# Sending the first unit's rows to the expert table one by one, with its routing closer behind its mLSTM

## The chip, the cores and the metric

The kernel runs on one core of a Trainium2 chip, in one launch. The metric is the time of an execution on the device in microseconds (us). Five engines work side by side, each through its own instructions in order: TensorE (PE, with its weight loads shown as PEld), VectorE (DVE), ScalarE (ACT), GpSimd (POOL) and SyncE (SP), which here only issues DMAs. POOL issues DMAs too, the indirect ones.

## The reference

One decoder layer over 16 sequences of 256 tokens with 256 channels, in float32:

```python
x = x + attention(layernorm(x), W_qkv, W_out)     # causal, 16 heads of 16 channels
x = x + mlstm(layernorm(x), ctx, ctx, ...)        # causal, 8 heads of 32 channels, gated decay
x = x + moe(layernorm(x), router_w, router_b, expert_up, expert_down)

def moe(x):                                       # 4096 tokens, 8 experts, hidden width 1024
    probs = softmax(x @ router_w + router_b)
    top_w, top_idx = top_k(probs, 2)
    comb = sum(top_w * one_hot(top_idx))
    return sum_e comb[:, e] * (gelu(x @ up[e].T) @ down[e].T)
```

Attention and mLSTM work sequence by sequence. The experts work on tokens: each token goes to two of the eight.

## The kernel before

**Stages.** The 16 sequences form two groups of 8 and four units of 4. The attention runs over `k`, a sequence times four quads of heads (64 in all, and four more values of `k` until the pipeline is empty): `attend_next(k)` computes the maxima of quad `k`, the weights of quad `k - 2` (scores `ps_st`, exponentials `p` on ACT, L408) and the values of quad `k - 4` (`ps_av`, L419 and L424). Between weights and values, `diagonals` (L340) applies the causal mask with two `affine_select` instructions on POOL (L343). The mLSTM's decay weights `d` pass through the same `diagonals`.

**The mLSTM and the routing** of a group are lists of steps that `mixing(group, slow)` (L915) writes out. A round `i` takes one half (four heads) of a sequence; `lags` (L961) says how many rounds later each step follows:

```python
end = [(4, finish), (2, values2)] if slow else [(2, values2), (3, finish)]
lags = ((1, scores2), *end, (5, layer3), (7, scale3), (8, turn3), (9, logits))
```

`finish` adds the mLSTM's result to x. `layer3` (L685) takes the statistics of the third layer norm and writes x to the output `out_x` by a DMA of SP's (L696). `scale3` (L702) normalizes x in place (L708, on POOL for the first group), and so must wait until that DMA has read it. `turn3` transposes it and `logits` multiplies it by the router (L727). When the last sequence of a unit has its logits, `logits_by_token`, `softmax3`, `choose` (a series of small DVE instructions) and `count` (`ps_n`, L797) give every token its two slots in a table in DRAM, one region for each expert.

**The table.** `send` (L826) is one indirect DMA on POOL (L827): 128 rows of 265 floats (the token, its expert weights and its number) to 128 slots. A unit has 8 tiles with two slots each, so 16 sends; `send_unit` (L837) does the two of one tile. After a unit's last send comes its `plan` (L846), which gives out blocks of 128 or 256 slots of an expert. `load_rows` (L1101) fetches a block's rows from the table; it must wait for the sends that came before its plan.

**What runs beside what.** The first group's attention runs alone (k = 0 to 35). Beside the second group's attention (k = 36 to 67), `take_evenly` (L1036) deals out the steps of the first group's mLSTM and routing, in equal numbers to each k, and ends two k before the attention's end (`EARLY`). `mixing` returns its list in parts. For the first group the cut `part` lies behind the first unit's plan; what is behind it (`kept`, L1059) is done after the attention, alternating with the first steps of the second group (`begin`, L1191). After the attention come the experts' blocks: 48 of them, each with up matmuls (`ps_u`, L1153), gelu, down matmuls (`ps_d`, L1171) and an indirect DMA that adds the result to the output (L1176). The steps of the second group are dealt out between their matmuls:

```python
parts = [(0, FIRST - 6, begin), (FIRST - 6, SECOND - 3, rest), (SECOND - 3, THIRD - 3, end)]
```

With FIRST = 9, SECOND = 13 and THIRD = 21, `begin` lies beside blocks 0 to 2, `rest` beside 3 to 9 and `end` beside 10 to 17. The remaining blocks run with no mLSTM beside them.

**Order on the engines.** In the stage of the blocks the orders of PE, ACT and SP are those of the program text. Everywhere else a planner puts the instructions of each engine in order at compile time, by the order of the text and by when its costs say that an instruction can start; a dependence between two instructions keeps their order. `bank`, `four` and others look at the list `singles`, which is empty until the attention is closed.

Of the kernel before, what the change touches and what calls it, by code (L numbers as in the profile page):

```python
# [34 lines left out]
UT = UB * SC  # L35
# [35 lines left out]
def decoder_layer(  # L71
# [15 lines left out]
    nc = tc.nc  # L87
# [65 lines left out]
    table = dram.tile([E * REGION + TB, ROW], F32, tag="table", name="table")  # L153
# [8 lines left out]
    def statistics(b, mv, rstd):  # L162

        for c in range(SC):
            st = lstm.tile([P, 6], F32, tag="st", name="st", bufs=4)
            nc.vector.bn_stats(st, xtile(b, c))
            nc.vector.bn_aggr(mv[:, c, :], st)
        nc.vector.tensor_scalar(rstd, mv[:, :, 1], LN_EPS, None, ALU.add)
        nc.scalar.activation(rstd, rstd, AF.Ln)
        nc.scalar.activation(rstd, rstd, AF.Exp, scale=-0.5)  # L170

    def normalized(xn, b, mv, rstd, engine=nc.gpsimd):
        for c in range(SC):
            engine.tensor_scalar(  # L174
                xn[:, c, :], xtile(b, c), mv[:, c, 0:1], rstd[:, c : c + 1], ALU.subtract, ALU.mult
            )
# [15 lines left out]
    singles = []  # L192
# [56 lines left out]
    for i in range(2):  # L249

        v = big.tile([P, SC, NA, HP], F32, tag=f"v{i}", name=f"v{i}")
# [26 lines left out]
    def step(f, *args):  # L278
        return lambda: f(*args)
# [3 lines left out]

    seq, quads = {}, {}

    def start1(b):
        mv = lstm.tile([P, SC, 2], F32, tag="mv1", name="mv1")
        rstd = lstm.tile([P, SC], F32, tag="rstd1", name="rstd1")
        statistics(b, mv, rstd)
        xn = lstm.tile([P, SC, D], F32, tag="xn", name="xn", bufs=3)  # L290
        normalized(xn, b, mv, rstd, nc.gpsimd if b else nc.vector)
        seq[b] = {"xn": xn}
# [47 lines left out]
    def diagonals(p):  # L340

        for block in (p[:, :, :P], p[:, :, S:]):
            nc.gpsimd.affine_select(  # L343
                out=block, in_=block, compare_op=ALU.is_ge, fill=0.0, base=0,
                pattern=[[0, 4], [1, P]], channel_multiplier=-1,
            )

    def maxima(k):

# [331 lines left out]
    routed = {}  # L681
# [144 lines left out]
    def send(place, row):  # L826
        i = nc.gpsimd.indirect_dma_start(  # L827
            out=table, out_offset=bass.IndirectOffsetOnAxis(ap=place, axis=0), in_=row, in_offset=None,
            bounds_check=E * REGION - 1, oob_is_err=False,
        )  # L830
        for other in sent:
            tc.declare_no_dep(i.ins, other, reason="the slots of any two rows differ")
        for other in fetched:
            tc.declare_no_dep(i.ins, other, reason="blocks given out before have no slot that was still free")
        sent.append(i.ins)

    def send_unit(u, c0, c1):  # L837
        g, t0 = divmod(u * UT, GB * SC)
        source = xs[g].rearrange("p b c r -> p (b c) r")
        for i in range(c0, c1):  # L840
            for k in range(2):
                send(routed[u]["place"][:, k, i : i + 1], source[:, t0 + i, :])

    plans, blk = {}, {}

# [69 lines left out]
    def mixing(group, slow):  # L915


        b0, b1 = group * GB, (group + 1) * GB
        ready = b0 + UB
        u = b0 // UB  # L920

        def pause(n):
            return [None] * (n if slow else 0)

        first = [step(load2, b) for b in range(b0, ready)] + [step(start2, b0)]
        for b in range(b0, ready):
            if b + 1 < ready:
                first.append(step(start2, b + 1))
            first.append(step(turn2, b))
        first += [step(gates, u), None, None] + pause(4) + [step(gates_out, u), step(gates_by_token, u), None]  # L930
        first += [step(maxima2, b0)] + pause(2)


        units = [[(b, dc) for b in range(v * UB, (v + 1) * UB) for dc in range(DC)] for v in (u, u + 1)]
        gap = [(None, None)] * (GAP if slow else 0)
        halves = units[0] + gap + units[1]
        n, n0 = len(halves), len(units[0]) + len(gap)
        second = {
            0: [(load2, ready), (start2, ready)],
            1: [(load2, ready + 1), (turn2, ready), (start2, ready + 1)],  # L940
            2: [(turn2, ready + 1), (start2, ready + 2)],
            4: [(load2, ready + 2), (turn2, ready + 2), (start2, ready + 3)],
            5: [(load2, ready + 3)],
            6: [(turn2, ready + 3), (gates, u + 1)],
        }
        if slow:
            second = {
                0: [(load2, ready)],
                1: [(load2, ready + 1)],
                4: [(load2, ready + 2)],  # L950
                6: [(load2, ready + 3)],
                8: [(start2, ready)],
                9: [(turn2, ready), (start2, ready + 1)],
                10: [(turn2, ready + 1), (start2, ready + 2)],
                11: [(turn2, ready + 2), (start2, ready + 3)],
                12: [(turn2, ready + 3)],
                17: [(gates, u + 1)],
            }
        second[n0 - 1] = [(gates_out, u + 1), (gates_by_token, u + 1)]
        end = [(4, finish), (2, values2)] if slow else [(2, values2), (3, finish)]  # L960
        lags = ((1, scores2), *end, (5, layer3), (7, scale3), (8, turn3), (9, logits))  # L961
        rest, outgoing, part = [], [], 0
        for i in range(n + 16):
            if i < n and halves[i][0] is not None:
                b, dc = halves[i]
                rest.append(step(decay, b, dc))
                if dc == DC - 1 and b + 1 < b1 and b + 1 != ready:
                    rest.append(step(maxima2, b + 1))
            for lag, f in lags:
                if not 0 <= i - lag < n or halves[i - lag][0] is None:  # L970
                    continue
                b, dc = halves[i - lag]
                if f in (scores2, values2):
                    rest.append(step(f, b, dc))
                elif dc == DC - 1:
                    rest.append(step(f, b))
                    if f is logits and (b + 1) % UB == 0:
                        v = b // UB
                        rest += pause(1) + [step(logits_by_token, v), step(softmax3, v)] + pause(1)
                        rest += [step(choose, v)] + pause(2) + [step(count, v)] + pause(1)  # L980
                        outgoing = [step(send_unit, v, c, c + 1) for c in range(UT)]
            for _ in range(min(2, len(outgoing))):
                rest.append(outgoing.pop(0))
                if not outgoing:
                    rest += [step(f, *args) for f, *args in plans_of[v]]
                    part = part or len(rest)
            rest += [step(*x) for x in second.get(i, [])]
            if i == n0 - 1:
                rest.append(step(maxima2, ready))
        return first, rest[:part], rest[part:]  # L990


# [48 lines left out]
    for k in range(k0):  # L1041
# [6 lines left out]
    plans_of = [  # L1048
        [(lambda: plan(lstm, list(range(FIRST)), P),)],
        [(lambda: plan(moe, list(range(FIRST, SECOND)), TB),)],  # L1050
        [(lambda: plan(moe, list(range(SECOND, THIRD)), TB),), (lambda: make_pads(),)],
        [
            (lambda: send_pads(),), (lambda: plan(moe, pairs, TB),), (lambda: plan(moe, rests, P, True),),
            (lambda: make_room(),),
        ],
    ]
    gathers, spreads = reorder(0)
    first, rest, end = mixing(0, False)
    steps, kept = gathers + spreads + first + rest, end  # L1059
    all_steps = len(steps)  # L1060
# [14 lines left out]
    def make_pads():  # L1075

        pad = moe.tile([P, ROW], F32, tag="pad", name="pad", bufs=1)
        unused.append(pad)
        nc.gpsimd.memset(pad, 0.0)
        nc.vector.tensor_copy(pad[:, D + E :], numbers[:, 0, :1])  # L1080
        i = nc.sync.dma_start(out=table[E * REGION : E * REGION + P], in_=pad)
        for other in sent + fetched:
            tc.declare_no_dep(i.ins, other, reason="these rows are behind all regions")
# [100 lines left out]
    def make_room():  # L1184
        mixers.close()
        late.append(ctx.enter_context(tc.tile_pool(name="late", bufs=AHEAD + 1, reuse_waits="tile")))

    first, rest, end = mixing(1, True)
# [111 lines left out]
```

## Time and profile before

| what | value |
|---|---|
| times of three runs | 1198.41 us median (1187.74 to 1206.18) |
| the profiled execution | 1186.61 us, span 1184.9 us |
| granted TensorE clock, mean | 0.931 of full speed |
| busy: PE, DVE, ACT, POOL | 1088.4, 609.7, 457.4, 396.0 us |
| last mask of the attention | at 531.8 us |
| sends of unit 0 (16) | from 510.2 to 531.8 us |
| sends of unit 1 (16) | from 577.0 to 597.4 us |
| sends of unit 2 (16) | from 711.5 to 731.8 us |
| one send on POOL, median | 0.975 us, to landing 2.8 us |

The span runs from the first to the last instruction of one execution. Busy time is the time in which an engine had an instruction in work; register, branch, semaphore and DMA-issuing instructions aren't counted. The granted clock is the share of full speed that TensorE had. In lists of waits, "A <- B" says that A's engine stood before A until B was done. Lines such as L827 are lines of the kernel before.

### The profile page before, as it was taken

Reading aid. Unit: us, or ns where it says so; the run is one execution under the profiler, and the core shown is the slowest. Engines: PE = TensorE matmul, PEld = TensorE weight load, DVE = VectorE, ACT = ScalarE, POOL = GpSimd, SP = SyncE. Lnnn points to the kernel's source line nnn. Section 1 sums busy time; section 2 is a strip of 40 time slices with the busy share of each in tenths; the row PEclk is TensorE's granted clock in tenths of the full one; section 3 lists DMA queues with packets and bytes.
Section 4 is the critical chain, followed back from the end, with each engine's and each line's share of the span. In section 5 each row is a group of like instructions: output and inputs, shape, how many; then the busy total and the mean of one; then the engine's idle time right before and its main releaser. Section 6 shows DMA issues by size and latency. Waiting matters only on the chain.

```text
span 1184.9 us, 23523 instructions
## 1 busy us (share of the span) xinstructions
PE 1088.4 (92%) x8814; PEld 851.2 (72%) x8814; DVE 609.7 (51%) x1651; ACT 457.4 (39%) x928; POOL 396.0 (33%) x446
## 2 busy tenths in 40 slices
PE   5999999998998999867879879999999999999997
PEld 4667777765665656546767667777888999999996
DVE  4778787666676656734737746475551111111110
ACT  2344444435563645322357544744421111111111
POOL 5233332153452433461443016312173222222222
PEclk9799999978998978768889999999999999999999
DMA  6200000002202201026187456644479988788841
GB/s 194 63 21 11 18 14 18 13 6 79 90 26 94 99 20 28 20 75 240 61 300 267 139 183 234 196 159 142 149 261 310 334 275 261 257 272 254 254 127 23
DMA packets 61202, 165.46 MB, mean 140 GB/s; under 512 B 11552, under 2 KB 42144, under 8 KB 46752
## 3 DMA queue, kind: packets, MB, share of 16 engines
q1 hardware_dynamic: 47296, 144.45, 34.9%
q0 software_dynamic: 13248, 18.69, 7.7%
q8 instruction: 72, 1.18, 0.4%
q10 hardware_dynamic: 544, 0.79, 0.2%
q14 instruction: 42, 0.34, 0.1%
HBM read 136.30 MB, written 23.14 MB: 135 GB/s over the span
## 4 chain that ended last, share of the span: by engine, by line
PE 57%; DMA 18%; DVE 9%; issue 8%; POOL 4%; ACT 3%; SPq 0%; POOLq 0%; ACTq 0%; DVEq 0%
DMA out_x<-y,to 14%; PE ps_d L1171 9%; PE ps_u L1153 8%; PE ps_qk L311 5%; PE ps_s L359 5%; PE ps_st L400 4%; PE ps_v L331 3%; PE ps_h L634 3%; PE ps_av L419 3%; PE ps_t L183 2%; PE ps_sc L611 2%; PE ps_st L404 2%; PE ps_g L541 2%; DMA rows<-table 1%; PE ps_s L364 1%
## 5 line engine op out<-in xcount | busy, mean ns | idle before, releaser
L1153 PE MATMUL ps_u<-xt,up 128*128 128x128 f32 (+1 forms) x1536 | 251.2, 321 | 0.5 <-DVE xt L1133 0.5
L1171 PE MATMUL ps_d<-down,h 128*128 128x256 f32 x1088 | 245.0, 381 | 0.0
L1153 PEld LDWEIGHTS ps_u<-xt,up 128*128 128x128 f32 x1536 | 225.3, 192 | 20.7 <-issue 1.9
L1171 PEld LDWEIGHTS ps_d<-down,h 128*128 128x128 f32 x1088 | 203.9, 191 | 27.5 <-issue 1.2
L1176 POOL DMA_INDIRECT out_x<-y,to x68 | 105.6, 1553 | 330.9 <-DVE y L1175 183.6
L343 POOL TENSOR_SCALAR_AFFINE_SELECT p<-p 128x512 f32<-128x512 f32 x128 | 78.9, 642 | 181.2 <-ACT p L408 143.0
L1159 ACT ACTIVATE h<-ps_u 128x512 f32<-128x512 f32 x78 | 46.6, 598 | 232.1 <-PE ps_u L1153 232.1
L408 ACT ACTIVATE p<-ps_st 128x768 f32<-128x768 f32 x128 | 98.7, 810 | 87.6 <-PE ps_st L404 87.4
L373 DVE TENSOR_TENSOR less<-mask_a,ps_s 128x512 f32<-128x512 f32 x128 | 86.8, 678 | 36.7 <-PE ps_s L364 36.6
L359 PE MATMUL ps_s<-kt,qt 16*128 16x256 f32 x512 | 84.9, 445 | 9.7 <-DVE d L620 5.9
L400 PE MATMUL ps_st<-qt,kt 32*128 32x256 f32 x512 | 79.0, 461 | 13.6 <-DVE off L377 12.4
L1175 DVE TENSOR_SCALAR y<-ps_d,wt 128x256 f32<-128x256 f32 x68 | 32.5, 479 | 106.0 <-PE ps_d L1171 105.9
L827 POOL DMA_INDIRECT table<-x,place x64 | 63.5, 992 | 67.2 <-DVE cnt L867 27.2
L378 DVE TENSOR_REDUCE mxs<-less 128x8 f32<-128x1024 f32 x64 | 77.3, 1208 | 0.0
L311 PE MATMUL ps_qk<-xnt,wqk_sb 128*128 128x256 f32 x256 | 71.5, 427 | 6.0 <-ACT xnt L298 2.9
L343 POOL TENSOR_SCALAR_AFFINE_SELECT d<-d 128x512 f32<-128x512 f32 x64 | 40.6, 683 | 96.9 <-ACT d L602 83.2
L620 DVE SCALAR_TENSOR_TENSOR d<-ps_sc,d 128x384 f32<-128x384 f32 (+1 forms) x96 | 60.3, 682 | 22.0 <-POOL d L343 13.9
L174 POOL TENSOR_SCALAR xn<-x,mv,rstd 128x256 f32<-128x256 f32 x46 | 56.3, 1235 | 44.5 <-PE ps_t L183 26.5
L602 ACT ACTIVATE d<-mb,at 128x256 f32<-128x256 f32 x128 | 63.7, 498 | 16.2 <-DMA mb<-mm 16.2
L1133 DVE COPY xt<-ps_r 128x256 f32<-128x256 f32 (+1 forms) x48 | 25.5, 531 | 85.8 <-PE ps_r L1131 85.6
L1136 DVE TENSOR_TENSOR w<-rows,one 128x8 f32<-128x8 f32 (+1 forms) x48 | 8.1, 169 | 112.1 <-DMA rows<-table 110.6
L311 PEld LDWEIGHTS ps_qk<-xnt,wqk_sb 128*128 128x128 f32 x256 | 51.3, 211 | 18.0 <-issue 3.6
(228 smaller groups left out, 1674.4 us busy)
## 6 DMA issues: line engine op xcount, KB each, us to landing
up<-in_wup SPq DMA_DIRECT2D x48, 1024.0 KB
down<-in_wdown SPq DMA_DIRECT2D x48, 1024.0 KB
mb<-mm SPq DMA_DIRECT2D x16, 1024.0 KB
rows<-table SPq DMA_DIRECT2D x20, 265.0 KB
x<-in_x SPq DMA_DIRECT2D x16, 256.0 KB
kt<-qt SPq DMA_DIRECT2D x128, 32.0 KB
qt<-rowed SPq DMA_DIRECT2D x256, 1.0 KB
cin<-in_ctx SPq DMA_DIRECT2D x16, 256.0 KB
```

The source lines that it names most:

```text
L311: nc.tensor.matmul(ps[:, i, :], lhsT=wqk_sb[:, dc, n : n + 4].rearrange("p n j h -> p (n j h)"), rhs=xnt[:, dc, :], start=dc == 0, stop=dc ...
L343: nc.gpsimd.affine_select(out=block, in_=block, compare_op=ALU.is_ge, fill=0.0, base=0, pattern=[[0, 4], [1, P]], channel_multiplier=-1,)
L359: nc.tensor.matmul(ps[h // 2][:, h % 2, P : P + S], lhsT=qt[channels(h), quad, P:], rhs=kt[channels(h), quad, :], start=True, stop=True,)
L373: nc.vector.tensor_tensor(less[:, part], mask_a[:, None].to_broadcast([P, 2, SC, P]), p.rearrange("p h (c k) -> p h c k", c=SC)[:, :, :, : ...
L378: nc.vector.tensor_reduce(mx[:, :, :4].rearrange("p c h -> p h c"), less, AX.X, ALU.min)
L400: nc.tensor.matmul(ps[h][:, :S], lhsT=kt[rows(h), quad, :P], rhs=qt[rows(h), quad, :], start=True, stop=True)
L408: nc.scalar.activation(p[:, part, :], x_, AF.Exp, scale=1.0 / math.sqrt(HA))
L602: nc.scalar.activation(d[:, h, :S], mb[:, n, :], AF.Exp, bias=at[:, 0, j, n : n + 1], scale=-1.0)
L827: i = nc.gpsimd.indirect_dma_start(out=table, out_offset=bass.IndirectOffsetOnAxis(ap=place, axis=0), in_=row, in_offset=None, bounds_chec ...
L1153: nc.tensor.matmul(ps[:, j, :], lhsT=m["up"][:, dc, f * P : (f + 1) * P], rhs=m["xt"][:, dc, :t], start=dc == 0, stop=dc == DC - 1,)
L1171: nc.tensor.matmul(ps, lhsT=m["h"][:, f, c * P : (c + 1) * P], rhs=m["down"][:, f, :], start=f == 0, stop=f == FC - 1)
L1176: a = nc.gpsimd.indirect_dma_start(out=acc, out_offset=bass.IndirectOffsetOnAxis(ap=m["to"][:, c : c + 1], axis=0), in_=y, in_offset=None, ...
```

## The change

For a group that runs beside the attention (not `slow`), the steps of layer3 to logits of the sequences of the first unit follow one to two rounds sooner. A send is now a step of its own (`send_tile`); up to four of the first unit's sends a round are spread among the round's other steps, and from the round after the logits on. Every send beside the attention depends on the latest mask that was written out before it. And the cut of the first group's list is moved from behind the first unit's plan to the end of round 23 of 32. The second group's steps keep their order, and its sends count singly.

```diff
+    pace = [None]
...
     def diagonals(p):
 
         for block in (p[:, :, :P], p[:, :, S:]):
-            nc.gpsimd.affine_select(
+            i = nc.gpsimd.affine_select(
                 out=block, in_=block, compare_op=ALU.is_ge, fill=0.0, base=0,
                 pattern=[[0, 4], [1, P]], channel_multiplier=-1,
             )
+        pace[0] = i.ins
...
     def send(place, row):
...
+        if pace[0] is not None and not singles:
+            tc.add_manual_dep(
+                i.ins, pace[0].name, mybir.DependencyInfo(mybir.DependencyClass.Sync, mybir.DependencyReason.DATA),
+                reason="rows go to the table one by one",
+            )
...
-    def send_unit(u, c0, c1):
+    def send_tile(u, i, k):
         g, t0 = divmod(u * UT, GB * SC)
         source = xs[g].rearrange("p b c r -> p (b c) r")
-        for i in range(c0, c1):
-            for k in range(2):
-                send(routed[u]["place"][:, k, i : i + 1], source[:, t0 + i, :])
+        send(routed[u]["place"][:, k, i : i + 1], source[:, t0 + i, :])
...
         lags = ((1, scores2), *end, (5, layer3), (7, scale3), (8, turn3), (9, logits))
-        rest, outgoing, part = [], [], 0
+        sooner = ((1, scores2), *end, (4, layer3), (5, scale3), (6, turn3), (7, logits))
+        rest, outgoing, part, v = [], [], 0, u
         for i in range(n + 16):
+            at, waiting = len(rest), len(outgoing)
...
-            for lag, f in lags:
+            for lag, f in [(lag, f) for both in zip(lags, sooner) for lag, f in sorted(set(both))]:
                 if not 0 <= i - lag < n or halves[i - lag][0] is None:
                     continue
                 b, dc = halves[i - lag]
+                if (lag, f) not in (lags if slow or b >= ready else sooner):
+                    continue
...
-                        outgoing = [step(send_unit, v, c, c + 1) for c in range(UT)]
-            for _ in range(min(2, len(outgoing))):
+                        outgoing = [step(send_tile, v, c, k) for c in range(UT) for k in range(2)]
+
+            among = not slow and v == u
+            now, some = rest[at:], min(4, waiting if among else len(outgoing))
+            del rest[at:]
+            for j in range(some):
+                rest += now[j * len(now) // some : (j + 1) * len(now) // some] if among else now if j == 0 else []
                 rest.append(outgoing.pop(0))
-                if not outgoing:
-                    rest += [step(f, *args) for f, *args in plans_of[v]]
+            if not some:
+                rest += now
+            elif not outgoing:
+                rest += [step(f, *args) for f, *args in plans_of[v]]
+                if slow:
                     part = part or len(rest)
             rest += [step(*x) for x in second.get(i, [])]
             if i == n0 - 1:
                 rest.append(step(maxima2, ready))
+            if not slow and i == n + n // 2 - 1:
+                part = len(rest)
         return first, rest[:part], rest[part:]
```

## The prediction

> **What bounds the kernel now.** I read the page's slices first, then the windows of four microseconds around the end of the attention, then the order of POOL there, then the waits, and last the order of PE behind the attention. The kernel is bound by TensorE nearly everywhere (PE is busy for 92% of the span), so a change pays only where PE stands or runs at half clock. The windows (start:end, length, busy time and instruction count of PE, PEld, DVE, ACT and POOL, granted clock, DMA share, GB/s) show one such place:
>
> ```profile
> 504.00:508.00 4.00, 4.00 (x19) 3.98 (x20) 0.34 (x3) 0.00 (x0) 0.00 (x0) 0.50 0.00 1
> 516.00:520.00 4.00, 4.00 (x47) 2.30 (x40) 1.46 (x10) 1.73 (x4) 3.09 (x4) 0.99 0.31 111
> 520.00:524.00 4.00, 2.55 (x32) 1.40 (x30) 1.16 (x3) 2.71 (x7) 3.52 (x5) 1.00 0.21 77
> 524.00:528.00 4.00, 1.11 (x19) 0.52 (x17) 0.39 (x1) 0.37 (x1) 3.09 (x4) 0.79 0.30 104
> 528.00:532.00 4.00, 0.00 (x0) 0.00 (x0) 0.00 (x0) 0.00 (x0) 3.08 (x5) 0.50 0.29 104
> 532.00:536.00 4.00, 1.51 (x16) 0.55 (x16) 0.49 (x2) 0.49 (x2) 3.40 (x4) 0.50 0.43 92
> ```
>
> From 520 to 536 PE works 5.2 of 16 us while POOL alone is full. POOL's order in time names what fills it:
>
> ```profile
> 501.77 1.22 POOL L343 TENSOR_SCALAR_AFFINE_SELECT p<-p 128x512 f32<-128x512 f32 x2 [1.84 <-ACT p L408]
> 510.21 1.23 POOL L827 DMA_INDIRECT table<-x,place  x1 [7.21 <-DVE cnt L867]
> ...
> 519.52 0.97 POOL L827 DMA_INDIRECT table<-x,place  x1 [0.30 <-issue]
> 520.49 1.23 POOL L343 TENSOR_SCALAR_AFFINE_SELECT p<-p 128x512 f32<-128x512 f32 x2
> 521.90 0.98 POOL L827 DMA_INDIRECT table<-x,place  x1 [0.17 <-issue]
> ...
> 530.86 0.97 POOL L827 DMA_INDIRECT table<-x,place  x1 [0.31 <-issue]
> 531.84 1.24 POOL L343 TENSOR_SCALAR_AFFINE_SELECT p<-p 128x512 f32<-128x512 f32 x2
> 533.03 1.28 POOL L675 TENSOR_TENSOR sq<-sq,gain 128x512 f32<-128x512 f32 x1
> ```
>
> Eight sends, one mask, eight sends, the last mask: the sixteen sends of unit 0 take 1.28 us each from start to start. The exponentials of the last two quads end at 512.7 and 523.2, so their masks start 7.8 and 8.6 us late. The waits from 494 to 560 show who pays:
>
> ```profile
> POOL x L708 <- DMA out_x<-x: 16.0, 1, 16.0
> ...
> PEld ps_av L419 <- POOL p L343: 8.2, 2, 7.4
> ...
> PE ps_av L419 <- POOL p L343: 7.2, 1, 7.2
> ```
>
> The 16.0 us are scale3 of the last sequence of group 0. Its x is ready at 535.5, but SP stands behind the first row load (which waits for the sends until 533.5) and then behind load_down(0), and writes out_x only at 547.55. Routing of unit 1 hangs on that, and behind the attention PE waits twice more, once for that routing's choice and once for the masks of group 1:
>
> ```profile
> 570.96 0.66 PE L797 MATMUL ps_n<-sel,earlier 128*128 128x64 f32 x2 [4.54 <-DVE sel L784]
> ...
> 610.96 1.22 PE L611 MATMUL ps_sc<-qt,ct 32*128 32x256 f32 x2 [7.23 <-DVE d L620]
> ```
>
> **The change part by part.** I counted the lists by hand. Beside the attention 150 steps become 165, still spread over k = 36 to 65; the part kept for the blocks goes from 21 to 22 (7 steps of routing leave it, 8 sends become 16 steps). Group 1's lists grow from 78 and 68 to 86 and 76, only because each send_unit is now two steps.
>
> *The sends of unit 0.* Before they lie at k = 62 to 65; after at k = 58 to 64, at most three to a k, each tied to the latest mask. Three take 3.8 us; sixteen before the end took 20.5. The instructions, their DMAs (2.8 us to landing at the median) and the queue stay the same. What a tied send waits for is an instruction ahead of it on POOL's own queue; behind it stand the next masks, and values waits for them. From 510.2 to 538.1 PE's own work, each group at its full-clock row, is about 14 us: eight groups of ps_av, ps_o and ps_st at 1.1, ps_h 1.4, four transposes at 0.66, logits 1.0 and 0.4 of a group begun. The stretch is 27.9 us, so 13.5 are lost. Some 4 us of these stay, since at the very end nothing covers exponential (1.5), mask (1.2), ps_av (1.1), copy (0.4). So **-9.5 us**; bounds -13.5 (all hidden) and 0 (another chain ends as late).
>
> *The steps that move into the attention.* layer3, scale3, turn3 and logits of sequences 5 to 7: on PE two transposes at 0.66 and two logits at 1.03, 3.4 us; on ACT two copies of 0.59 and two of 0.36; on POOL two scalings of 1.22; on DVE two statistics of 0.4 and less; on SP one out_x write, now ahead of the row loads and of load_down(0). In the attention I charge **+0.5 us**, since most of PE's 3.4 fall into the 4 us just left open; without that cover they cost 3.4. Behind the attention they free more than they weigh: logits(7) comes at 558.3 and the choice ends at 570.9; after it, logits(7) can go at once, some 11 us sooner, so the choice (11 us from logits on) lies under the spreads and the up matmuls of block 0 (3.8). What is late next is DVE: spreads, statistics, normalization, copies, choice and plan keep it at 4.00 of 4 from 560 to 568. Without the wait of 4.54 and with half of ps_n's 4.0 us at clock 0.50, the gates start **-8 us** relative to the attention's end; bounds -13 (the second wait, 7.23, shrinks too) and 0 (the two scratch DMAs of 6.4 us each end where they end now, because the 1 MB weight loads hold the DMA share near 1.0 from 592 on).
>
> *Closer lags for sequences 0 to 3.* No instruction is added. scale3 comes one round behind layer3, not two, and finish one round ahead of it. The masks that queue behind a waiting scale3 are the price; see the rival. I charge 0, because layer3's write (6.8 us) fits into a round of about 13 us (1.3 k of 10 us); bounds -4 (the choice of unit 0 meets more work of other kinds at k = 58 than at k = 62, half of the 8.6 us that PE loses from 494.6 to 510.2) and +24.
>
> *The finer steps of group 1.* The same order, but the steps ahead of the sends are dealt out about a tenth sooner, and each block has that much less matmul to cover them. Between 600 and 720 PE stands for 19 of 120 us, so **+3**; bounds 0 and +9 (a tenth of the 100 us up to the first send of unit 2).
>
> *The planner.* Except for the blocks' PE, ACT and SP, the order on an engine is made at compile time from costs. No view shows what it will make of the new list. The stretches at half clock inside the attention (412 to 424) show that a misplaced group costs 4 to 6 us: I take 0, bounds -6 and +6.
>
> Sum: -9.5 + 0.5 - 8 + 3 = **-14 us**. The profiled execution took 1186.6 us (span 1184.9 and 1.7 around it), which would become 1172.6. The median of the runs shown lies 11.8 higher, at 1198.4; against it the forecast is **1184 us**, a ratio of 0.988.
>
> A rule weighed against the rows: the granted clock is 0.50 from 496 to 516 and 528 to 540, although PE counts as busy for all of 504 to 508. The Trainium skill, "TensorE: Matmul & The Clock Gate", Part 1, says that TensorE falls to half rate after an idle window of about 3.4 us and needs about as long of sustained work to return. By that rule filling the gap also speeds the work behind it; an estimate from that page takes some 3 us more off the sum. The trace agrees on the size of the step, and shows it also where PE counts as busy with few, dependent matmuls.
>
> **The rivals.**
> 1. *More is freed: about -28, 1170 us.* With the gap and the chain of the choice covered, the half-clock stretches go too. From 492 to 516 PE is busy 21.6 us, mostly at 0.50; at full clock it would need half, -10; ps_n at 572 to 580 gives 4 more. For it: every one of these stretches follows a chain that moves. Against it: the choice still sits in PE's order with DVE working in series.
> 2. *The gain is eaten: about -3, 1195 us.* finish(7) at k = 62, its write, scale3(7) and turn3(7) at k = 65 (2.4 + 1.5 + 7 + 2.4 + 1.3 us, and more on full queues) end as late as the last mask did; or the scratch and weight DMAs fix the start of group 1. For it: the DMA share near 1.0. Against it: from 564 to 576 the DMAs are idle.
> 3. *Slower: about +24, 1222 us and more.* POOL stands in order behind scale3. Three of the seven scalings in the attention already wait for the out_x write, 8.9 us in all; at 456.5 it is 5.64 us, two masks stand behind it, and the window from 456 to 464 has 48 matmuls at clock 0.66 where its neighbours have 72 to 104. With one round between write and scaling, eight scalings that each wait the write's full 6.8 us delay the masks by some 4.8 beyond the 2 us of slack: +38, less the 14. It decides from about six waits of over 5 us. Against it: a round is twice the write.
>
> That the pacing does nothing (the planner puts the sends in two heaps again) is part of rival 2: a tie to a later mask forbids the first heap, not a second one.
>
> **How the numbers follow.** The forecast gets 0.43, more freed 0.25, eaten 0.13, slower 0.19. Its own range is 1172 to 1198. To leave out no more than 2 in 10 the range goes from 1152 (half of the freed case's further bounds) to 1224. A measurement of this kernel can tell about 2%, 24 us, from no change, so faster means under 1174 and slower over 1222. Faster: 0.25 and a twentieth of the forecast's, 0.30. Slower: 0.19. Same: 0.51.
>
> **What would show it.** Right: no more than four sends between two masks, no PE wait for a mask above 2 us in the last 30 us of the attention, granted clock near 1.0 there, no POOL wait of 16 us for out_x, logits(7) within 6 us of the spreads' start, the masks of group 1 some 17 us sooner. Wrong: waits of scale3 for out_x that add up to over 30 us and fall inside the attention (rival 3); PE idle as before but for another reason in the last 20 us (rival 2); or a loss between 620 and 850, where only the finer steps act.

## The result, and the profile after

Over fifteen runs of each kernel the median is 1185.73 us after the change (1175.93 to 1191.02) and 1193.93 us before it (1185.81 to 1206.18). The ratio is 0.9947 with an interval of [0.9923, 0.9971]: half a per cent, well inside the 2% that the prediction called no change. On another chip, where both kernels take longer, the ratio is 1.0009 [0.9983, 1.0035].

The profiled execution after took 1187.03 us (span 1185.3, mean granted clock 0.927). That of before (1186.61) lies 7.3 us below its own median, this one 1.3 above its own, so the two spans do not differ although the medians do by 8 us. The traces are therefore compared stage by stage. Four stages are read off POOL's order in time: the attention ends where the tile `pad` is cleared, the first POOL instruction behind the last `ps_o`; then come the first mask `d` of group 1, the twentieth indirect add to the output, and the end. In the tables, sends are given by the start of the first and of the last.

| kernel | sends of unit 0 | last mask done | attention ends | to first mask of group 1 | from there to add 20 | add 20 to the end |
|---|---|---|---|---|---|---|
| before | 510.2–530.9 | 533.1 | 538.2 | 70.8 | 233.9 | 342.0 |
| after | 480.7–521.1 | 529.0 | 541.3 | 58.0 | 244.0 | 342.0 |

So the attention ends 3.1 us later, the stage behind it is 12.8 us shorter, and the stage with group 1's mLSTM beside the blocks is 10.1 us longer. That is the whole difference of the spans.

POOL's order at the end of the attention, after the change (start, duration, instruction, and in brackets the idle time before it with what ended it):

```profile
514.57 1.22 POOL L345 TENSOR_SCALAR_AFFINE_SELECT p<-p 128x512 f32<-128x512 f32 x2 [1.63 <-ACT p L411]
...
521.12 0.99 POOL L830 DMA_INDIRECT table<-x,place  x1 [0.28 <-POOL p L345]
526.60 0.62 POOL L345 TENSOR_SCALAR_AFFINE_SELECT p<-p 128x512 f32<-128x512 f32 x1 [4.50 <-ACT p L411]
...
529.02 1.08 POOL L680 TENSOR_TENSOR x<-x,sq 128x512 f32<-128x512 f32 x1
```

The two heaps of eight sends are gone: never more than three stand between two masks, behind each mask the first send is released by it, and where a mask waits, it now waits for its exponentials. What the change says of the sends, it does. PE counts as busy for 11.7 of the 16 us from 520 to 536, where it was for 5.2. But it is busy mostly at half clock, and with a gap (columns as in the prediction's windows):

```profile
524.00:528.00 4.00, 3.18 (x22) 1.73 (x22) 0.99 (x3) 2.30 (x5) 1.40 (x2) 0.50 0.00 0
528.00:532.00 4.00, 1.23 (x3) 0.38 (x4) 1.14 (x5) 0.60 (x2) 2.10 (x3) 0.50 0.24 70
532.00:536.00 4.00, 3.27 (x10) 1.09 (x8) 0.00 (x0) 1.25 (x4) 1.36 (x2) 0.50 0.79 246
```

The clock is 0.50 from 524 to 536, and from 528 to 532 PE has three matmul records in 4 us. PE's own order in time names what stands in the gap:

```profile
530.77 1.88 PE L730 MATMUL ps_l<-xt,wrout_sb 128*8 128x256 f32 x4 [3.19 <-ACT xt L718]
...
534.43 1.88 PE L730 MATMUL ps_l<-xt,wrout_sb 128*8 128x256 f32 x4 [0.73 <-ACT xt L718]
...
536.75 1.06 PE L422 MATMUL ps_av<-p,v 128*32 128x256 f32 x2
```

The last mask is done at 529.04, yet the last two groups of `ps_av` start only at 536.75, because two `logits` stand ahead of them in PE's order, and the first of these waits for `xt`. This copy of `turn3` (L718) went into the place of the tag `"sq"`, of which there is one, and which `finish` uses for its squares (L667). The last reader of that place is the add of POOL's L680 that ends at 530.10, in the fence above: `finish` of the last sequence. The waits of this stretch list it as ACT `xt` L718 <- POOL `x` L680, 2.1 us. From the last mask to the end of the attention it takes 12.3 us, before 5.2.

Behind the attention, the group 1 masks start at 599.30, before at 609.00; the wait of 4.54 us for the choice is gone, and that of 7.23 us for the masks is 3.39. The gates of group 1 start 33.7 us behind the attention's end, before 43.0 (PE's order, before and after):

```profile
581.22 1.46 PE L541 MATMUL ps_g<-qt,wg 128*32 128x256 f32 x15
```

```profile
575.03 1.46 PE L544 MATMUL ps_g<-qt,wg 128*32 128x256 f32 x15
```

The chain that ended last, between 640 and 690, runs differently in the stage after that (start, duration, step):

```profile
640.67 3.67 PE ps_d L1192 x16
...
645.46 5.56 DMA rows<-table
...
659.68 5.77 PE ps_d L1192 x16
...
666.65 6.45 DMA rows<-table
```

Twice the row load of a later block begins only 1.1 to 1.2 us after a block's down matmuls end, and the chain runs through the whole load. SP's order explains the place: `load_down` stands directly ahead of `load_rows` there (issues at 644.35 and 645.46, at 665.47 and 666.65), and goes out when the down matmuls end. A third such load follows at 808.86 (5.55 us). The three make 17.6 us, or 7.2% of the chain of this stage. Before, the chain of the same stage has one:

```profile
632.53 4.76 DMA rows<-table
```

The order on SP is not new: before, every row load of this stage follows a `load_down` directly too, this one issued at 632.53 behind one at 631.36. Nor is a load's length in the chain its price, since PE goes on with other matmuls during it. What waits is DVE, for the weights `w` of that block, 3.06 us at the first and 1.63 at the second. The waits and the windows of the whole stage, before and after:

```profile
DVE w L1136 <- DMA rows<-table: 11.1, 6, 4.3
...
609.00:843.00 234.00, 215.77 (x1716) 170.25 (x1717) 140.82 (x391) 128.39 (x258) 61.76 (x66) 0.97 0.57 188
```

```profile
DVE w L1157 <- DMA rows<-table: 12.8, 9, 3.2
...
599.30:843.30 244.00, 219.88 (x1720) 173.33 (x1720) 141.44 (x397) 129.88 (x259) 61.78 (x65) 0.94 0.55 183
```

Of the 10 us more, PE is busy for 4.1, at a lower mean clock, and stands for 5.9; DVE's waits for rows grow by only 1.7.

### The profile page after: what moved, and what is told of

It is laid out like the page before. It is cut to its first block, busy times and chain, and to the rows that moved or that the text cites. A ratio compares the mean times of both kernels' runs of the same rounds, so it can differ in the third digit from the quotient of the medians.

```text
span 1185.3 us, 23511 instructions
## 1 busy us (share of the span) xinstructions
PE 1086.4 (92%) x8814; PEld 852.5 (72%) x8814; DVE 607.5 (51%) x1651; ACT 457.4 (39%) x928; POOL 394.9 (33%) x446
## 4 chain that ended last, share of the span: by engine, by line
PE 43%; DMA 16%; DVE 7%; issue 6%; ACT 3%; POOL 3%; SPq 0%; POOLq 0%; DVEq 0%; ACTq 0%
DMA out_x<-y,to 12%; PE ps_d L1192 11%; PE ps_u L1174 9%; PE ps_h L637 3%; DMA rows<-table 3%; PE ps_sc L614 2%; PE ps_st L403 2%; PE ps_t L183 2%; PE ps_qk L313 2%; PE ps_s L362 2%; PE ps_av L422 1%; PE ps_l L730 1%; PE ps_g L544 1%; PE ps_v L333 1%; POOL out_x L1197 1%
## 5 line engine op out<-in xcount | busy, mean ns | idle before, releaser
L1192 PE MATMUL ps_d<-down,h 128*128 128x256 f32 x1088 | 248.2, 384 | 0.0
L403 PE MATMUL ps_st<-qt,kt 32*128 32x256 f32 x512 | 82.3, 470 | 17.3 <-DVE off L380 12.8
L313 PE MATMUL ps_qk<-xnt,wqk_sb 128*128 128x256 f32 x256 | 74.5, 440 | 5.7 <-ACT xnt L300 2.9
L403 PEld LDWEIGHTS ps_st<-qt,kt 32*128 32x128 f32 x512 | 37.1, 204 | 44.9 <-issue 27.4
```

What stands on the lines that cost most here:

```text
L313: nc.tensor.matmul(ps[:, i, :], lhsT=wqk_sb[:, dc, n : n + 4].rearrange("p n j h -> p (n j h)"), rhs=xnt[:, dc, :], start=dc == 0, stop=dc ...
L403: nc.tensor.matmul(ps[h][:, :S], lhsT=kt[rows(h), quad, :P], rhs=qt[rows(h), quad, :], start=True, stop=True)
L1192: nc.tensor.matmul(ps, lhsT=m["h"][:, f, c * P : (c + 1) * P], rhs=m["down"][:, f, :], start=f == 0, stop=f == FC - 1)
```

## The experiments

Each kernel ran beside the kernel before on its chip; e1 to e4 ran on one chip, e5 to e12 on another. On both, the kernel before takes 3.6% longer than on the first (medians 1236.4 to 1238.2 us), so ratios are compared, and stages only among these kernels. The stages are those of one execution each: that of e5 lies 7.5 us above its kernel's median, that of e10 7.2, that of e12 6.1, the others at most 3.4 from theirs. Cut and lags are those of the diff.

| kernel | ratio to before | sends of unit 0 | attention ends | to first mask of group 1 | from there to the end |
|---|---|---|---|---|---|
| e5, before | 0.9996 [0.9961, 1.0031] | 513.6–534.3 | 545.8 | 83.8 | 614.8 |
| e6, after | 1.0009 [0.9983, 1.0035] | 481.2–522.5 | 541.1 | 74.5 | 621.4 |
| e1 | 1.0126 [1.0075, 1.0177] | 515.0–545.2 | 549.2 | 83.0 | 618.6 |
| e2 | 1.0052 [1.0022, 1.0082] | 478.4–498.9 | 546.1 | 73.7 | 620.3 |
| e3 | 0.9915 [0.9887, 0.9943] | 501.8–526.8 | 545.8 | 72.8 | 609.4 |
| e4 | 0.9916 [0.9883, 0.9948] | 478.6–520.1 | 539.5 | 72.4 | 611.7 |
| e7 | 1.0093 [1.0056, 1.0130] | 478.5–499.1 | 555.6 | 75.3 | 620.0 |
| e8 | 0.9847 [0.9785, 0.9908] | 469.1–520.6 | 529.5 | 72.8 | 619.9 |
| e9 | 0.9778 [0.9725, 0.9831] | 471.9–517.5 | 525.0 | 74.0 | 610.9 |
| e10 | 0.9859 [0.9811, 0.9907] | 510.4–531.1 | 541.8 | 78.5 | 611.0 |
| e11 | 0.9833 [0.9787, 0.9880] | 497.6–523.4 | 539.1 | 72.5 | 611.7 |
| e12 | 1.0014 [0.9983, 1.0046] | 516.0–546.4 | 550.3 | 83.0 | 612.7 |

### The parts one by one: e1 to e4

**e1, only the sends one by one.** The changed kernel with the old lags and the old cut:

```diff
-        sooner = ((1, scores2), *end, (4, layer3), (5, scale3), (6, turn3), (7, logits))
+        sooner = lags
...
-                if slow:
-                    part = part or len(rest)
+                part = part or len(rest)
-            if not slow and i == n + n // 2 - 1:
-                part = len(rest)
```

> One part alone: the first unit's rows go one by one, each tied to the latest mask, and the lags and the cut stay as in the kernel before. Theory A (the sends pay at the end of the attention, and what they gain there is spent by the steps that the change moves into the attention, whose transposes and logits pass one after the other through one buffer): no mask late, no moved steps, so the attention ends 6 to 9 us sooner than before, and the time is 0.992 to 0.995 of before. Theory B (the time comes from the cut alone: routing of the second unit goes sooner, the sends do nothing): 1.000, with the attention's end where it was.

Measured: 1.0126, slower by more than one per cent, which neither theory had. With the old lags the sends can't start before 515, and spread out they last until 545.2; the attention ends 3.4 us later than in e5, the stage behind it is as long as before, and the blocks lose 3.8. Alone, the sends one by one gain nothing.

**e2, everything but the sends one by one.** The changed kernel, with the sends neither spread nor tied:

```diff
-        if pace[0] is not None and not singles:
+        if False:
...
-            among = not slow and v == u
+            among = False
```

> The change without the one-by-one part: closer lags and the later cut stay, the sends follow each round's steps four at a time and without a tie. Theory A: masks late again at the place where the sends now lie, so the attention ends 5 us or more later than with the whole change, group 1's first mask comes within 3 us of before, and the time is 0.998 to 1.002 of before. Theory B: the same as the whole change, 0.993 to 0.997.

Measured: 1.0052, above both theories. The sends go out as four and then twelve, the last at 498.9 and 36 us before the last mask; still the attention ends at 546.1, as late as before, and 6.6 us later than in e4, whose sends are spread. But no mask waits behind the twelve sends. At their time ACT stands for 14.5 us ahead of `ht` with no releaser in the trace (e4: 4.7 us), and the first chip shows no such pause (see the last section); so these 6.6 us are not shown to be the price of late masks.

**e3, only the cut.** The kernel before, with the first group's list cut at the end of round 23:

```diff
-                    part = part or len(rest)
+                    if slow:
+                        part = part or len(rest)
...
+            if not slow and i == n + n // 2 - 1:
+                part = len(rest)
```

> The cut alone: the steps of rounds 20 to 23 go into the attention, lags and sends as before. Theory A: the attention ends 3 to 6 us later than before (late masks, and the chain through one buffer on top), the routing of unit 1 comes 10 us sooner behind it, net 0.997 to 1.002. Theory B: 0.993 to 0.997, all of what the whole change gives.

Measured: 0.9915, a larger gain than either theory had. The attention ends where it did, the stage behind it is 11.0 us shorter than in e5. This one part is worth more than the whole change in e6 (1.0009, on the other of these two chips); against the first chip's 0.9947 the intervals overlap.

**e4, group 1 in pairs again.** The changed kernel, but the second group sends both slots of a tile in one step, as before:

```diff
+    def send_pair(u, i):
+        for k in range(2):
+            send_tile(u, i, k)
...
+                        if slow:
+                            outgoing = [step(send_pair, v, c) for c in range(UT)]
...
-            now, some = rest[at:], min(4, waiting if among else len(outgoing))
+            now, some = rest[at:], min(2 if slow else 4, waiting if among else len(outgoing))
```

> The whole change, but the second group's sends are dealt out in pairs again, so that its lists have 78 and 68 steps as before. Theory A (the finer steps take cover away from group 1's mLSTM: 3 us, at most 9): 0.990 to 0.993 of before, the loss between 620 and 800 us gone. Rival (the loss there comes from row loads that stand behind weight loads in SP's queue, whatever the grain): the same as the whole change, 0.993 to 0.997.

Measured: 0.9916, as Theory A had it. From the first mask of group 1 to the end it takes 611.7 us; the changed kernel takes 621.4 (e6, on the other chip). The finer steps cost over 8 us. The chain holds one row load between group 1's first mask and the twentieth add, where e2 on the same chip has three, at 665.34, 686.43 and 842.51, of 5.5 to 7.1 us. The count goes with the cost in the kernels with fine steps (three in each), but e3, e5 and e11, with pairs, have two, and e3's time to the end is the shortest of all; so the count does not show the cause.

### The same pair, the tie and the shared place: e5 to e8

**e5 and e6, the two kernels unchanged.**

> The kernel before, profiled again beside the others of this call, so that their stages can be set against its own on the same chip. Expected: ratio 0.998 to 1.002; the attention's end (the clearing of the pad tile on POOL) near 538 us and the two heaps of eight sends as in the first profile, since the order on the engines is fixed; if blocks and attention differ from the first profile, the difference is the chip's or the execution's, not a kernel's.

> The changed kernel, profiled again beside the others of this call. Theory A (the later cut frees the start of group 1, and the ties keep the closer lags from costing): attention's end within 3 us of before on the same chip, group 1's first mask 8 to 13 us sooner, 0.990 to 0.996 of before. Theory B (the gain sits in the blocks, not behind the attention): first mask within 3 us of before.

Measured: 0.9996 and 1.0009; for the changed kernel both theories had a gain. On this chip the attention does end sooner after the change, by 4.7 us (545.8 to 541.1), not later; but the after side ends at the same time on both chips (541.3 and 541.1), and it is the before side that moved, from 538.2. Its trace here has a pause of 10.6 us of ACT ahead of `ht` that the first chip's has not (see the last section), and it is the slowest of ten executions. Behind the attention it is 9.3 us shorter, and from group 1 on 6.6 longer.

**e7, without the tie.** The changed kernel with only the dependence on the latest mask left out; the steps are dealt out one by one as in the change:

```diff
-        if pace[0] is not None and not singles:
+        if False:
```

> The whole change without the dependence on the latest mask; the sends stay spread in the list. The planner then lets 13 of the 16 sends run in one heap. Theory A (the tie is what keeps the closer lags and the finer list from costing): masks some 15 us late behind the heap, the attention's end 5 to 8 us later than with the tie, as without the whole one-by-one part, ratio 1.000 to 1.006 of before. Theory B (what costs is the position of the sends in the list, not the heap): as with the tie, 0.990 to 0.996.

Measured: 1.0093, beyond both theories. POOL's order in time, and ACT's:

```profile
499.07 0.98 POOL L830 DMA_INDIRECT table<-x,place  x1 [0.30 <-issue]
510.28 1.28 POOL L678 TENSOR_TENSOR sq<-sq,gain 128x512 f32<-128x512 f32 x1 [10.23 <-DVE sq L676]
...
512.86 1.22 POOL L345 TENSOR_SCALAR_AFFINE_SELECT p<-p 128x512 f32<-128x512 f32 x2
```

```profile
495.92 0.58 ACT L643 COPY ht<-ps_h 128x512 f32<-128x512 f32 x1 [12.18 <-remote]
```

The planner puts three sends and then thirteen together (483.70 to 499.07). No mask starts between 482.29 and 512.86, and the attention ends 14.5 us later than in e6. Dealing the steps out singly is not enough; the tie is what spreads the sends. But no mask waits behind the thirteen: POOL itself then stands for 10.23 us, and the next mask's exponentials start only at 509.07. At the time of the sends ACT stands for 12.18 us with no releaser in the trace. e6 has no such pause in its attention, and the first chip has none at all, so what the tie is worth there was not measured.

**e8, a place of its own for `xt` of the routing.** The changed kernel with one line changed: the copy of `turn3` goes into the three places of the normalized x (tag `"xn"`), and so waits neither for `finish` nor for the `logits` of the sequence before:

```diff
-        xt = lstm.tile([P, DC, S], F32, tag="sq", name="xt3", bufs=1)
+        xt = lstm.tile([P, DC, S], F32, tag="xn", name="xt3", bufs=3)
```

> The whole change, but the transposed rows of turn3 go into the three buffers of the normalized x (free at that time) and no longer into the one that finish uses for its squares. Theory A (at the attention's end turn3 and logits of sequences 4 to 7 pass one by one through that buffer, behind finish(7), and the last two value groups stand behind them in PE's order): the wait of 3.2 us ahead of logits(5) goes, half-clock windows from 520 to 540 shrink, the attention ends 4 to 8 us sooner than with the change, ratio 0.986 to 0.991 of before. Rival (the end is fixed by finish(7), its write and scale3(7)): the same end within 2 us, ratio as the change's.

Measured: 0.9847, more than Theory A had. The attention ends at 529.5, 11.6 us sooner than in e6 on the same chip, and the other stages stay within 2 us. Of the 11.6 us, 7.6 lie between the last mask and the end (5.0 us, in e6 12.6), and 4.0 ahead of it. The shared place is what held the end of the attention; whether the other tag or the number of places frees it was not tried apart.

### The repairs together, and what each part is then worth: e9 to e12

**e9, e4 and e8 together.** Both edits above in the changed kernel.

> The whole change with both repairs: turn3's rows in the buffers of the normalized x, and the second group's sends in pairs, so that its lists have 78 and 68 steps again. Theory A (the two losses are separate: the chain at the attention's end, and group 1's lists being dealt out too soon): the gains of the two add up, 0.974 to 0.982 of before; the attention ends near 529 us and the stretch from group 1's first mask to the twentieth added tile is 250 to 254 us. Rival (the two overlap): 0.983 to 0.988.

Measured: 0.9778, as Theory A had it, the lowest ratio here, faster than both the kernel before and the changed one. From group 1's first mask to the end it takes 9.0 us less than e8, from which it differs in the pairs alone. In its trace a window reads

```profile
516.00:520.00 4.00, 3.40 (x43) 1.91 (x41) 0.00 (x0) 3.00 (x6) 3.46 (x5) 1.00 0.09 34
```

and PE's order has

```profile
517.72 1.03 PE L730 MATMUL ps_l<-xt,wrout_sb 128*8 128x256 f32 x4
...
520.37 1.03 PE L730 MATMUL ps_l<-xt,wrout_sb 128*8 128x256 f32 x4 [0.68 <-ACT xt L718]
```

The two `logits` that in the changed kernel waited 3.19 and 0.73 us and took 1.88 each wait 0 and 0.68 here and take 1.03, at full clock. By the rule that the prediction weighed (the Trainium skill, "TensorE: Matmul & The Clock Gate", Part 1), filling a gap also speeds the work behind it; these rows agree. The changed kernel's half clock isn't only that gap's, though: its clock is 0.61 already from 520 to 524, where PE counts as busy for all of 4 us and no wait of PE from 516 to 524 is above 1.1.

**e10, the kernel before with only that place.** The one line of e8 in the kernel before.

> The kernel before with turn3's rows in the buffers of the normalized x, nothing else. Theory A (the chain through one buffer hurts mainly the steps that the change moves into the attention's end): 0.993 to 1.000 of before, since the two heaps of sends still hold the last masks. Rival (the shared buffer is the cost, whatever the change): 0.984 to 0.990, as in the changed kernel with the own place.

Measured: 0.9859, as the rival had it. The shared place cost the kernel before as well: the attention ends 4.0 us sooner than in e5, the stage behind it is 5.3 shorter, and the rest 3.8. This ratio can't be told from e8's 0.9847: where the place is free, the change as it was made adds nothing that shows.

**e11, the cut and that place.** e3 with the line of e8.

> The later cut alone with turn3's rows in the buffers of the normalized x: lags, sends and the grain of group 1 as before. Theory A (the ties and closer lags are needed to take the sends off the last masks): 0.986 to 0.993 of before, attention's end 6 us or more behind that of the whole change with the own place. Theory B (cut and own place are all that is needed): 0.974 to 0.982.

Measured: 0.9833, between the two theories. Against e9 it lacks the sends one by one and the closer lags; the intervals of the two overlap, so what these are worth once the place is free (0.55% by the ratios) is not certain. The stages speak for it: the attention of e11 ends at 539.1, that of e9 at 525.0, and e9 gives back only 0.7 of these 14.1 us later. But ACT has pauses without a releaser of 7.5 and 2.4 us in e11's attention and none in e9's, so this is the worth on this chip.

**e12, e1 with group 1 in pairs.** The sends one by one with nothing else of the change.

> One by one alone, as in the first run of these, but the second group's sends in pairs, so that its lists have 78 and 68 steps as before. Theory A (of the 1.3% that one by one alone lost, two thirds are the finer steps of group 1, and the rest lies at the attention's end, where the tied sends are still under way when the last masks come): 1.000 to 1.006 of before. Rival (the loss is the ties' alone): 1.010 to 1.015.

Measured: 1.0014, as Theory A had it. Of the 1.26% that e1 lost, 1.1% were the finer steps of group 1. In the attention the spread sends last until 546.4, and the last `logits` there waits 4.74 us for the copy into the shared place.

## Why the prediction was right or wrong, point by point

The forecast of 1184 us lies beside the measured median of 1185.73, but that is luck, not its steps: the sum of -14 us was made against the first three runs' median of 1198.4, and over fifteen runs it is 1193.9. In the profiled pair the terms add up to nearly nothing: the attention's two terms failed, the one behind it held and more, and the one for group 1 was mis-sized. (The chance of faster, 0.25 and a twentieth of 0.43, is 0.27, not 0.30.)

**The sends of unit 0, -9.5: the step that failed.** The heaps went as forecast, and no wait of PE for a mask is left among the waits of that stretch. But the attention ends 3.1 us later in the first pair and 4.7 sooner in e5 and e6. The 13.5 us that PE lost were put down to the masks alone, and the bound of 0 ("another chain ends as late") was right where the value taken was not. That chain is `finish`, `turn3` and `logits` of the last sequences through one place for `sq` and `xt`, with PE's last `ps_av` in order behind it. e8 shows it: with other places the attention ends 11.6 us sooner, 7.6 of them behind the last mask. The prediction had read that `turn3` and `logits` move into this stretch, and counted their instructions, but not the buffers they share with `finish`.

**The moved steps, +0.5.** They were said to fall into time left open, and to cost 3.4 us without that cover. They are the steps that stand ahead of `ps_av`: the two `logits` at half clock take 1.88 us each instead of 1.03, and wait 3.19 and 0.73. How much of the 3 us by which the attention ends later is theirs and how much the shared place's can't be told apart, since they are the same steps.

**Behind the attention, -8: right.** The term was stated for the gates, and relative to the attention's end they start 9.3 us sooner. The first mask of group 1 comes 12.8 us sooner, near the bound of -13, as the second wait shrinks too (7.23 to 3.39 us). e3 does this part alone and gains 11.0 there; the kernels with the old cut (e1, e5, e12) need 83.0 to 83.8 us for this stage (78.5 with the other place, e10), those with the new one 72.4 to 75.3. The forecast that these masks come some 17 us sooner in absolute time (they come 9.7) failed only by the attention's end.

**The finer steps of group 1, +3: mis-sized.** The stage takes 10.1 us longer in the first pair, above the bound of +9. On the two other chips, from the first mask of group 1 to the end, the five kernels with fine steps take 618.6 to 621.4 us and the seven with pairs 609.4 to 614.8; the means are 620.0 and 611.7, a cost of 8.3. e8 and e9, on one chip, differ by 9.0. That the finer steps cost this is shown; by which wait is not. The prediction spread the loss evenly over PE's idle time, and in the first pair PE does stand for 5.9 us more, but it is also busy for 4.1 more at a mean clock of 0.94 instead of 0.97, which the term left out. The chain holds 17.6 us of row loads in this stage against 4.8 before, but DVE's waits for rows grow from 11.1 us to 12.8 only.

**The closer lags, 0, and the rival of +24.** `scale3` waits once for the write of `out_x` between 235 and 545, for 8.1 us; before it was 8.9 in three waits:

```profile
POOL x L711 <- DMA out_x<-x: 8.1, 1, 8.1
```

This rival didn't come, as was argued. Without the tie e7's attention ends 14.5 us later, at least in part by a pause that the first chip doesn't show, so what the lags cost without it stays open.

**The planner, 0 within 6.** With the tie, its order costs nothing that shows. Without it the two heaps become one of thirteen, so the case that the pacing does nothing is excluded; its price on that chip, 14.5 us, was beyond the bound.

**The rivals.** "The gain is eaten" came nearest: about -3 by `finish`, write, scaling and `turn3` of the last sequence ending as late as the last mask did. These steps did end as late, but by a buffer, not by the write's time; and 7 us more than the term had were eaten in group 1. The forecast's own landmarks fell the same way: sends, waits for masks, the 16 us wait and the last sequence's `logits` (547.34, 0.6 us behind the spreads' start) as foretold; the clock near 1.0 in the last 30 us not (0.50 from 524 to 536); and PE idle for another reason at the attention's end and the loss between 620 and 850, both named as what would make it wrong, are there.

**What stays open.** Why the medians of the first chip differ by 8 us when its profiled pair doesn't differ by stages: the kernel before was profiled in one of its shortest executions, and which stage is longer in the others no trace here shows. Also open are which wait carries the cost of the finer steps, and what the tie is worth on the first chip.

## What to carry to other kernels

Before crediting the removal of a wait, list what else must pass the same engine in order before the stage can end, and for every step that a change moves there look up the buffers it takes and who read them last: here one tile with one place cost 11.6 us, in the attention that the change was to shorten. A list that is dealt out in equal numbers is re-timed by every step that is added to it, far from where the edit was meant to act. A step's length in the chain is not yet what it costs: look at what waits for it. And do each part of a change alone: one of three parts (the cut, 0.9915) was worth more than all together in e6 (1.0009).

## What the runs showed of the hardware that was not expected

The same kernel takes 1194 us on one chip and 1237 on two others. On those two, ACT and DVE stand for long times with nothing in the trace that releases them; the waits call such a releaser remote. ACT's order in time in e6:

```profile
583.46 0.58 ACT L536 COPY qt<-ps_t 128x512 f32<-128x512 f32 x1 [14.39 <-remote]
```

This pause lies in the heap of unit 1's sixteen sends (560.6 to 580.9) and ends 2.6 us after the last of them, and PE waits behind it for 13.2 us. Later, from 891 to 913 us, PE has a row of gaps of up to 1.6 us put down to issue, while POOL issues the sends of unit 3 and of the pads. The waits with a remote releaser add up to 95.7 us on ACT and DVE in e6 and 105.1 in e5; in the first chip's traces of both kernels there is none. They come with the heaps of indirect DMAs. Inside the attention the longest is 7.5 to 14.5 us where the sends of unit 0 stand in heaps (e2, e3, e5, e7, e10, e11), and where they are spread there is none (e1, e6, e9, e12) or one of about 5 (e4, e8). How much of the 43 us they explain is not shown, nor why one chip has them and another not.
